# Spatial attentions of a four-layer image kernel: inverse sums spread by transposes, an output projection folded into the value weights, division in place in PSUM

## The chip, the cores and the metric

The kernel runs on one core of a Trainium2 chip. The metric is the time of one execution in microseconds; smaller is better. The core has TensorE (PE in the profile, with its weight loads shown apart as PEld), VectorE (DVE), ScalarE (ACT) and GpSimd (POOL). SyncE (SP) issues most of the DMA transfers, ACT some. All engines run their own instruction streams in order and wait for each other by semaphores.

## The reference, cut to what matters

All data are float32. Four layers run one after the other on `x` of shape (2, 128, 64, 64), so N = 4096 positions for each of two images: a state-space layer (layer 0), an attention over positions with 3x3 convolutions for queries, keys and values and a 1x1 output projection (layer 1), an attention with 1x1 projections (layer 2), and a multi-scale layer (layer 3). The two attentions are what the change touches:

```python
# layer 1
q = conv2d(x, Wq, bq, 1).reshape(b, c, n)
k = conv2d(x, Wk, bk, 1).reshape(b, c, n)
v = conv2d(x, Wv, bv, 1).reshape(b, c, n)
attn = softmax(einsum('bci,bcj->bij', q, k) * c ** -0.5, axis=2)
out = einsum('bij,bcj->bci', attn, v).reshape(b, c, h, w)
out = conv2d(out, Wo, bo, 0)            # 1x1
x = x + out
# layer 2
q, k, v = (einsum('dc,nci->ndi', w_, xf) + b_ for w_, b_ in ((wq, bq), (wk, bk), (wv, bv)))
attn = softmax(einsum('nci,ncj->nij', q, k), axis=-1)
x = gamma * einsum('ncj,nij->nci', v, attn) + x
```

The output projection of layer 1 is linear in the channels, as the values' convolution is, and the softmax's division is a factor for each query.

## The kernel before, in words

Layer 0 is written as 32 chunks of 512 positions (two images, two inner layers, eight chunks); each chunk is 32 slots long. `background(i)` lists by hand which steps are emitted in which slot beside the scan of chunk i: step functions are given to `at(slot, function, ...)`, and within a slot they are emitted in the order listed. The loop over chunks begins at i = -2, so that chunk 0 is prepared ahead. During i = -1 nothing is scanned yet: `load_rest` (slot 1, L175) issues the loads of the raw 3x3 weights of layer 1 (`raws`, three tiles for queries, keys and values) and of the second image; `prepare(1)` is emitted in slot 7 (L156); `fold(k)` in slots 8 to 10 (L190) makes on VectorE, out of a raw weight tile, the weights of a one-dimensional Winograd form of the convolution; `fold_out` (slot 23, L208) writes them to DRAM. The same slots hold the first chunk's own path: silu on ScalarE (slot 11, L332), `xproj` (slot 13), `spread_bc` (slot 14, DMAs through DRAM), `soft_plus` (slot 17), `dt_end` on GpSimd (slot 18), `spread_dtu` (slot 19), `times_b` (slot 26, L389) and then the first scans (L407). Matmul outputs of these steps share two PSUM buffers (`mm`, tag "mm").

The attentions are four runs, `runs = [(0,0),(0,1),(1,0),(1,1)]` as (layer, image). A run has 128 units; eight units make a group of 256 queries (`QG`), 16 groups a run. Each pass `now` of the loop at L904 emits one unit's scores (`score`, L749: two matmuls of 128x512 and one VectorE instruction that copies them out of PSUM and takes their maxima), the products of the unit 14 passes earlier (`product`, L803: four matmuls of 128x256 that accumulate into `po`), and what falls due by `w = now % 8`: exponentials on ScalarE (w 3 and 7), `turn` (w 1, 5 and 3, 7; L776: row sums and reciprocals, a 32x32 block transpose on VectorE, and copies or DMAs that bring the blocks to their places), and the end of a group. Queries, keys and values of layer 1 go through `products` and `outputs` (L647, L668); `values` also turns the values by 128x128 transposes (`turned`, L713).

A group ends like this. `diagonals` (w 2, L811) makes on VectorE two 128x128 diagonal matrices out of the identity and the reciprocals `rec` of the row sums. `spread` (w 3, L816) multiplies a matrix of ones by each, so that the reciprocals lie along the columns and are the same on all partitions; ScalarE copies the result out (`rb`). `divide` (w 5, L832) multiplies `po` by `rb` into an SBUF tile `on`, and in layer 2 adds `gamma * on` to the image. In layer 1, `finish_mm` (w 7, L838) multiplies `on` by the output projection into `p2`, and `finish` (L843) adds `p2` and the bias `bo1` to the image:

```python
dg = sta["dg", it] = sp.tile([P, P], F32, name="dg", tag="dg", bufs=2)
nc.vector.tensor_scalar(dg, ident, sta["rec", r, grp][:, it : it + 1], None, ALU.mult)
nc.tensor.matmul(pr[:, it * P : (it + 1) * P], lhsT=ones, rhs=sta["dg", it], start=True, stop=True)
nc.tensor.matmul(sta["p2", r, grp], lhsT=wa[:, WS_O : WS_O + C], rhs=sta["on", r, grp], start=True, stop=True)
```

`pr` and `p2` share one PSUM buffer (`psm`, tag "m"); `po` has two (`psa`, tag "acc"), and scores two of 128x1024 (`pss`).

Of the kernel before, what the change touches and what calls it, by code (L numbers as in the profile page):

```python
# [6 lines left out]
F32 = mybir.dt.float32  # L7
AF = mybir.ActivationFunctionType
ALU = mybir.AluOpType
# [4 lines left out]
B, C, H, W = 2, 128, 64, 64  # L14
N = H * W
P = 128
# [43 lines left out]
WS_O, WS_Q, WS_K, WS_V, WS_IN, WS_OUT, WS_FUS = 0, 128, 256, 384, 512, 896, 1024  # L60
# [7 lines left out]
def tile_conv_seq(ctx: ExitStack, tc, x, consts, vecs, wemb, wlay, wconv, wdt, wqkv, wsmall, wms, out):  # L68
    nc = tc.nc

    kp = ctx.enter_context(tc.tile_pool(name="const", bufs=1))
# [11 lines left out]
    def rows(ap):  # L83
        return ap.rearrange("p (h w) -> p h w", w=W)
# [15 lines left out]
    ident = kc[:, K_ID : K_ID + P]  # L100
    cm = kc[:, K_CM : K_CM + P]
    ones = kc[:, K_ONE : K_ONE + P]

    def v1(name, i=0):
        return vec[:, VEC[name] + i : VEC[name] + i + 1]
# [10 lines left out]
    with tc.manual_schedule(), ExitStack() as s:  # L116
        wp = layers.enter_context(tc.tile_pool(name="l0w", bufs=1))
        spl = layers.enter_context(tc.tile_pool(name="l0t", bufs=1))
        mm = layers.enter_context(tc.tile_pool(name="l0mm", bufs=2, space=PSUM))
        yp = layers.enter_context(tc.tile_pool(name="l0y", bufs=1, space=PSUM))  # L120
        sp = scans.enter_context(tc.tile_pool(name="l0s", bufs=1, side="right"))
# [3 lines left out]

        we = wp.tile([P, 2, C], F32, name="we")
        nc.sync.dma_start(we, wemb)


        sel = wp.tile([P, 32], F32, name="sel")  # L130
# [14 lines left out]
        def load_layer(l):  # L145
            cw = sp.tile([P, KC + 1, DI], F32, name="cw", tag="h", bufs=5)
            nc.sync.dma_start(cw[:, KC, :], wlay[l][:, :DI])
            nc.sync.dma_start(cw[:, :KC, :].rearrange("p k d -> p (k d)"), wconv[l : l + 1, :].to_broadcast([P, KC * DI]))
            cws.append(cw)
            w = wp.tile([P, NWL - DI], F32, name=f"wl{l}")  # L150
            nc.sync.dma_start(w, wlay[l][:, DI:])
            d = wp.tile([R, DI], F32, name=f"wd{l}")
            nc.sync.dma_start(d, wdt[l])
            wl.append(w), wd.append(d)
# [18 lines left out]
        raws, folded = [], []  # L173

        def load_rest():  # L175
            for which in range(3):
                raw = sp.tile([P, 3, 3, C], F32, name="raw", tag="h", bufs=5)
                nc.sync.dma_start(raw.rearrange("p y x c -> p (y x) c"), wqkv[:, which])
                raws.append(raw)
            for c in range(NCH):  # L180
                load_x(1, c)
# [4 lines left out]
        for c in range(2, NCH):  # L186
            load_x(0, c)
        load_layer(1)

        def fold(which):  # L190

# [301 lines left out]
        def background(i):  # L493

            todo = [[] for _ in range(NSL)]

            def at(t, f, *a):
                todo[t].append((f, a))

            n, p, q, r = i + 1, i - 1, i - 2, i + 2  # L500
            if has(q):
                at(3, gelu, q)
                at(6, ffn_down, q, (0, 1)), at(7, ffn_down, q, (2, 3)), at(9, ffn_add, q)
                at(11, out_mm, q), at(12, out_add, q)
            if has(p):
                at(7, y_out, p, 1), at(7, gate, p)
                at(9, mix_out, p), at(11, mix_add, p)
            if has(n):
                at(0, pu_taps, n, 0, (0, 1)), at(1, pu_taps, n, 0, (2, 3)), at(2, pu_out, n, 0)
                at(3, pu_taps, n, 1, (0, 1)), at(4, pu_taps, n, 1, (2, 3)), at(5, pu_out, n, 1)  # L510
                at(13, xproj, n), at(14, xproj_out, n), at(14, spread_bc, n, 0), at(22, spread_bc, n, 1)
                at(15, dtproj, n, 0), at(16, dtproj, n, 1), at(17, soft_plus, n), at(18, dt_end, n)
            if has(i):
                at(1, pz_mm, i, 0), at(3, pz_out, i, 0)
                at(5, pz_mm, i, 1), at(6, pz_out, i, 1)
            if has(i) or has(n):
                at(11, silu, i, n)
            if i == -1:
                at(1, load_rest), at(7, prepare, 1)
                for k in range(3):  # L520
                    at(8 + k, fold, k), at(23, fold_out, k)
                at(19, spread_dtu, 0), at(26, times_b, 0)
            pair = [(k, second) for k, second in ((p, True), (r, False)) if has(k)]
            if has(r):
                at(10, embed, r), at(11, embed_out, r)
            w, m = {}, len(pair)
            for k, (it, second) in enumerate(pair):
                at(12 + 2 * k, ln_centre, w, k, it)
                at(13 + 2 * k, ln_square, w, k, it)
                at(27, ln_spread, w, k, m), at(28, ln_scale, w, k, it)  # L530
                at(29, ln_shift, w, k, it, second)
            if pair:
                at(17, ln_var, w, m), at(18, ln_eps, w, m), at(19, ln_rs, w, m), at(20, ln_newton, w, m), at(21, ln_step, w, m)
            if has(p):
                for f in range(4):
                    at(30 + f // 2, ffn_up, p, f)
            if has(i):
                at(24, y_out, i, 0)
            return todo
# [34 lines left out]
        wa = wbig.tile([P, NWA], F32, name="wa")  # L574
# [6 lines left out]
        QG = 256  # L581
        NB, NTH = P // 32, N // P // 2
        NU = 8 * N // QG
        LAG = 14
# [7 lines left out]
        runs = [(l, b) for l in range(2) for b in range(B)]  # L592
        sta = {}
# [2 lines left out]
            nc.scalar.activation(dst, src, AF.Identity, bias=bias)  # L596

        def bias(r, which):
            return v1("b" + "qkv"[which] + "12"[runs[r][0]])


# [206 lines left out]
                rhs = sta["pt", r, grp, jt // NTH][:, :, jt % NTH, :]  # L808
                nc.tensor.matmul(sta["po", r, grp], lhsT=sta["vt"][:, jt, :], rhs=rhs, start=(jt == 0), stop=(jt == N // P - 1))  # L809

        def diagonals(r, grp):  # L811
            for it in range(2):
                dg = sta["dg", it] = sp.tile([P, P], F32, name="dg", tag="dg", bufs=2)
                nc.vector.tensor_scalar(dg, ident, sta["rec", r, grp][:, it : it + 1], None, ALU.mult)

        def spread(r, grp):  # L816

            pr = psm.tile([P, QG], F32, name="pr", tag="m")
            for it in range(2):
                nc.tensor.matmul(pr[:, it * P : (it + 1) * P], lhsT=ones, rhs=sta["dg", it], start=True, stop=True)  # L820
            rb = sta["rb", r, grp] = sp.tile([P, QG], F32, name="rb", tag="rb", bufs=2)
            nc.scalar.copy(rb, pr)

        def xg(r, grp):
            l, b = runs[r]
            if l:
                k = QG // W
                return xt[:, b, 1 + grp * k : 1 + (grp + 1) * k, 1 : W + 1]
            cc, i = divmod(grp, 4)
            return xt[:, b, 1 + 16 * cc : 17 + 16 * cc, 1 + i : W + 1 : 4]  # L830

        def divide(r, grp):  # L832
            on = sta["on", r, grp] = sp.tile([P, QG], F32, name="on", tag="on")
            nc.vector.tensor_tensor(on, sta.pop(("po", r, grp)), sta.pop(("rb", r, grp)), ALU.mult)
            if runs[r][0]:
                nc.vector.scalar_tensor_tensor(xg(r, grp), rows(on), v1("gamma"), xg(r, grp), ALU.mult, ALU.add)

        def finish_mm(r, grp):  # L838
            if not runs[r][0]:
                sta["p2", r, grp] = psm.tile([P, QG], F32, name="p2", tag="m")  # L840
                nc.tensor.matmul(sta["p2", r, grp], lhsT=wa[:, WS_O : WS_O + C], rhs=sta["on", r, grp], start=True, stop=True)

        def finish(r, grp):  # L843
            if not runs[r][0]:
                nc.vector.scalar_tensor_tensor(xg(r, grp), sta.pop(("p2", r, grp)).rearrange("p (h w) -> p h w", w=16), v1("bo1"), xg(r, grp), ALU.add, ALU.add)

        def in_turn(f, u0):

            r, u = divmod(now - u0, NU)
            if 0 <= r < len(runs):  # L850
                f(r, u)

        NALL = len(runs) * NU
# [47 lines left out]
        sp = s.enter_context(tc.tile_pool(name="ats", bufs=1, reuse_waits="tile"))  # L901
        psa = s.enter_context(tc.tile_pool(name="atpa", bufs=2, reuse_waits="tile", space=PSUM))
        psm = s.enter_context(tc.tile_pool(name="atpm", bufs=1, reuse_waits="tile", space=PSUM))
        for now in range(NALL + LAG + 10):  # L904
            r, u = divmod(now, NU)
            w = now % 8
            if now < NALL:
# [42 lines left out]
                elif u == LAG:  # L950
                    load(0, LO), load(0, HI)
                    if r == 0:
                        load(1, LO)
            if w == 7:
                in_turn(lambda r, u: finish_mm(r, u // 8), LAG + 9)
            in_turn(product, LAG)
            if w == 7:
                in_turn(lambda r, u: finish(r, u // 8), LAG + 9)
            if w in (3, 7):
                in_turn(lambda r, u: exponentials(r, u // 4), 3)  # L960
            if w in (1, 5):
                in_turn(lambda r, u: turn(r, u // 4, 0), 5)
            if w in (3, 7):
                in_turn(lambda r, u: turn(r, u // 4, 1), 7)
            if w == 2:
                in_turn(lambda r, u: diagonals(r, u // 8), 10)
            if w == 3:
                in_turn(lambda r, u: spread(r, u // 8), 11)
            if w == 5:
# [7 lines left out]
    with ExitStack() as s, tc.manual_schedule():  # L977
        sp = s.enter_context(tc.tile_pool(name="mss", bufs=1, reuse_waits="tile"))
        mm = s.enter_context(tc.tile_pool(name="msmm", bufs=3, reuse_waits="tile", space=PSUM))
# [493 lines left out]
```

## Time and profile before

| what | value |
|---|---|
| median of 3 runs | 4995.87 us (4994.74 to 4996.39) |
| span of the profiled execution | 4994.0 us |
| its own time | not listed beside the span; the three runs lie 0.7 to 2.4 us above the span, the median 1.9 us |
| PE busy | 4661.7 us, 93% of the span |
| DVE busy | 4022.4 us, 81% |
| ACT busy | 2358.4 us, 47% |
| POOL busy | 2335.3 us, 47% |
| mean granted TensorE clock | 0.950 |

The span is cut in 40 slices on the profile's page. Layer 0 takes about the first 2180 us, the attentions the stretch from there to about 4218 us, layer 3 the rest. In layer 0 DVE is at nine tenths or more in nearly all slices and PE at eight to nine; in the attentions PE is at nine tenths or more throughout and DVE at six to eight. "Busy" of a matmul is modelled and holds its latency, so the rate of a row of matmuls is read from the distances between starts in the timeline, and a float32 matmul that isn't a transpose counts as two instructions there.

### The profile page before, as it was taken

What the parts mean: (1) busy time and instruction counts of PE and PEld (TensorE: products, weight loads), DVE (VectorE), ACT (ScalarE), POOL (GpSimd) and SP (SyncE); (2) the same over time, 40 slices, a digit from 0 to 9 for tenths busy, and PEclk for the clock granted to TensorE, in tenths of its full rate; (3) what the DMA queues carried; (4) which work ended last, traced back from release to release, by engine and by line L of the source; (5) the groups of instructions that cost most, each with busy time, mean ns of one, the idle gap of its engine ahead of it and who ended that gap; (6) DMA issues with size and microseconds to landing.
All of it is one profiled execution on the core that took longest, in us unless ns stands there. A gap on an engine that the chain in (4) does not pass through costs nothing.

```text
span 4994.0 us, 48951 instructions
## 1 busy us (share of the span) xinstructions
PE 4661.7 (93%) x14797; PEld 2242.2 (45%) x14797; DVE 4022.4 (81%) x4283; ACT 2358.4 (47%) x3218; POOL 2335.3 (47%) x1974
## 2 busy tenths in 40 slices
PE   6898899899988899899999999999999999999997
PEld 2222222222222222366667766666666666333332
DVE  7999999999999999778886677767776775667776
ACT  4677777777777777532222222233233332323332
POOL 3777777666777777513332233323333332333331
PEclk7889998998999989899999999999999999999998
DMA  6233333332333333224444344434444443000000
GB/s 165 68 69 69 69 71 73 71 69 65 67 67 69 69 70 68 71 57 110 109 109 126 105 111 113 118 97 111 113 98 98 110 114 87 3 7 7 5 7 9
DMA packets 242343, 386.24 MB, mean 77 GB/s; under 512 B 88592, under 2 KB 88992, under 8 KB 233632
## 3 DMA queue, kind: packets, MB, share of 16 engines
q1 hardware_dynamic: 192928, 315.94, 26.1%
q10 hardware_dynamic: 49152, 67.17, 5.4%
q8 instruction: 118, 1.93, 0.2%
q14 instruction: 145, 1.19, 0.1%
HBM read 101.02 MB, written 13.37 MB: 23 GB/s over the span
## 4 chain that ended last, share of the span: by engine, by line
PE 46%; POOL 24%; issue 12%; DVE 9%; DMA 3%; SPq 2%; ACT 2%; ACTq 0%; DVEq 0%; POOLq 0%
POOL h L414 19%; PE po L809 13%; PE pq L759 13%; DVE tr L789 3%; DMA pt<-tr 3%; PE pa L656 2%; PE pf L1130 2%; SPq L800 2%; PE pqkv L1157 2%; PE pw L1216 1%; POOL dtu L374 1%; POOL z L437 1%; PE pb L656 1%; PE pfus L1281 1%; PE psc L1181 1%
## 5 line engine op out<-in xcount | busy, mean ns | idle before, releaser
L796 POOL COPY pt<-tr 32x512 f32<-32x512 f32 x1024 | 648.8, 634 | 1439.2 <-DVE tr L789 704.5
L411 DVE TENSOR_TENSOR_SCAN h<-da,carry,h 128x512 f32<-128x512 f32 x1024 | 1240.7, 1265 | 62.0 <-ACT da L400 31.8
L414 POOL TENSOR_TENSOR h<-h,cb 128x2048 f32<-128x2048 f32 x256 | 1160.8, 4535 | 20.7
L759 PE MATMUL pq<-k,q 128*128 128x512 f32 x2048 | 962.6, 593 | 6.9 <-DVE sc L764 6.9
L809 PE MATMUL po<-pt,vt 128*128 128x256 f32 x4096 | 965.6, 379 | 2.5 <-DMA pt<-tr 2.5
L774 ACT ACTIVATE sc<-sc,nm 128x2048 f32<-128x2048 f32 x256 | 510.5, 1995 | 914.9 <-DVE nm L770 685.8
L809 PEld LDWEIGHTS po<-pt,vt 128*128 128x128 f32 x4096 | 777.9, 190 | 294.8 <-issue 208.3
L764 DVE TENSOR_SCALAR_CACHE_REDUCE sc<-pq 128x1024 f32<-128x1024 f32 x512 | 624.7, 1221 | 315.4 <-PE pq L759 293.8
L400 ACT ACTIVATE da<-dtb,am 128x512 f32<-128x512 f32 x1024 | 681.4, 684 | 220.9 <-DVE h L411 207.6
L789 DVE STREAM_TRANSPOSE tr<-sc 128x2048 f32<-128x2048 f32 x256 | 591.6, 2311 | 65.6 <-DMA pt<-tr 56.3
L393 DVE TENSOR_TENSOR h<-bb,pdu 128x2048 f32<-128x2048 f32 x256 | 581.3, 2271 | 77.6 <-PE py L426 29.4
L426 PE MATMUL py<-h,sel 128*32 128x512 f32 x2048 | 510.8, 642 | 1.6 <-POOL h L414 1.6
L759 PEld LDWEIGHTS pq<-k,q 128*128 128x128 f32 x2048 | 382.9, 190 | 283.0 <-issue 247.2
L387 PE MATMUL pdu<-dtu,fsel 128*128 128x512 f32 x512 | 327.6, 726 | 103.0 <-DVE h L393 100.6
L426 PEld LDWEIGHTS py<-h,sel 128*32 128x32 f32 x2048 | 115.3, 118 | 415.9 <-issue 409.0
L314 PE MATMUL pu<-xn,wu 128*128 128x512 f32 x512 | 246.4, 615 | 7.2 <-ACT u L320 5.5
L387 PEld LDWEIGHTS pdu<-dtu,fsel 128*128 128x128 f32 x512 | 96.6, 215 | 310.2 <-DVE h L393 185.9
L413 POOL COPY carry<-h 128x4 f32<-128x4 f32 x256 | 47.7, 186 | 389.8 <-DVE h L411 389.8
L1223 DVE TENSOR_TENSOR ov<-v,pw 128x2048 f32<-128x2048 f32 x64 | 146.1, 2284 | 62.1 <-PE pw L1216 62.1
L1157 PE MATMUL pqkv<-f,ws 128*128 128x512 f32 x384 | 188.1, 615 | 3.0 <-DVE prod L1174 2.3
L1227 POOL TENSOR_TENSOR ov<-ov 128x2048 f32<-128x2048 f32 x16 | 72.5, 4534 | 235.7 <-DVE ov L1223 235.7
L374 POOL TENSOR_TENSOR dtu<-dt,u 128x1024 f32<-128x1024 f32 x32 | 75.2, 2350 | 188.7 <-ACT dt L368 188.7
(259 smaller groups left out, 5262.2 us busy)
## 6 DMA issues: line engine op xcount, KB each, us to landing
pt<-tr SPq DMA_DIRECT2D x2048, 64.0 KB, 2.0
dtb<-dt SPq DMA_DIRECT2D x1024, 64.0 KB, 2.0
pt<-tr ACTq DMA_DIRECT2D x1024, 64.0 KB, 2.2
bb<-dr SPq DMA_DIRECT2D x128, 256.0 KB, 4.4
cb<-dr SPq DMA_DIRECT2D x128, 256.0 KB, 4.7
uw<-ufold SPq DMA_DIRECT2D x12, 576.0 KB, 4.9
uw<-dkept SPq DMA_DIRECT2D x20, 288.0 KB, 3.1
xt<-in_x SPq DMA_DIRECT2D x16, 256.0 KB, 4.8
```

The costliest lines, as they stand in the source:

```text
L387: nc.tensor.matmul(pdu, lhsT=four(s_ % 4), rhs=st[i]["dtu"][:, s_ // 4, :], start=True, stop=True)
L393: nc.vector.tensor_tensor(h, st[i]["bc", 0], pdu.unsqueeze(1).to_broadcast([P, 4, CH]), ALU.mult)
L400: nc.scalar.activation(da, st[i]["dtb", s_], AF.Exp, scale=am[items[i][1]][:, j, gg, m : m + 1])
L411: nc.vector.tensor_tensor_scan(h[:, m, :], da, h[:, m, :], carries[b, l][:, j, gg, m : m + 1], ALU.mult, ALU.add)
L414: nc.gpsimd.tensor_tensor(h, h, st[i]["bc", 1], ALU.mult)
L426: nc.tensor.matmul(py[r : r + 32, :], lhsT=sel, rhs=st[i]["h", s_ + k][:, m, :], start=(m == 0), stop=(m == 3), tile_position=(0, r),)
L759: nc.tensor.matmul(pq[:, i, :], lhsT=sta["q", r, grp][:, it * P : (it + 1) * P], rhs=sta["k"][:, at : at + CH], start=True, stop=True)
L764: nc.vector.tensor_scalar(dst, pq, 1.0, None, ALU.mult, ALU.max, accum_out=sta["mx"][:, c2 : c2 + 1])
L774: nc.scalar.activation(sc, sc, AF.Exp, bias=nm, scale=scale, accum_out=sm[:, hh : hh + 1])
L789: nc.vector.transpose(tr, sta.pop(("sc", r, blk, hh)).rearrange("p (t r f) -> p r t f", r=NB, f=32))
L796: nc.gpsimd.tensor_copy(dst, src)
L809: nc.tensor.matmul(sta["po", r, grp], lhsT=sta["vt"][:, jt, :], rhs=rhs, start=(jt == 0), stop=(jt == N // P - 1))
```

## The change

In both attentions the inverse sums are spread by a transpose on TensorE of `rec` itself, read with a stride of zero over 128 columns; `diagonals` and its tiles are gone. `divide` multiplies `po` by `rb` in place in PSUM and then adds to the image straight from there, in layer 1 too. `finish_mm`, `finish` and `p2` are gone: the output projection of layer 1 is multiplied into the raw weights of its values' convolution, and into that convolution's bias (`bvo`), by a new step `through_out`, which is emitted in slot 9 of i = -1, after `prepare(1)` and before `fold(1)` and `fold(2)`. One load (`wo`, 64 KB) is added at the head of `load_rest`. The attention loop is two passes shorter.

```diff
         def load_rest():
+            nc.sync.dma_start(wo, wsmall[:, WS_O : WS_O + C])
             for which in range(3):
...
+        def through_out():
+
+            raw = raws[2].rearrange("p y x c -> p (y x) c")
+            for turn in (True, False):
+                for k in range(0, 9, 3):
+                    pv = mm.tile([P, 3, C], F32, name="pv", tag="mm")
+                    for i in range(3):
+                        if turn:
+                            nc.tensor.transpose(pv[:, i, :], raw[:, k + i, :], ident)
+                        else:
+                            nc.tensor.matmul(pv[:, i, :], lhsT=raw[:, k + i, :], rhs=wo, start=True, stop=True)
+                    nc.scalar.copy(raw[:, k : k + 3, :], pv)
+            pb = mm.tile([P, 1], F32, name="pbv", tag="mm")
+            nc.tensor.matmul(pb, lhsT=wo, rhs=v1("bv1"), start=True, stop=True)
+            nc.scalar.copy(bvo, pb)
...
-                at(1, load_rest), at(7, prepare, 1)
+                at(1, load_rest), at(7, prepare, 1), at(9, through_out)
...
         def bias(r, which):
+            if which == 2 and not runs[r][0]:
+                return bvo
...
-        def diagonals(r, grp):
+        def spread(r, grp):
+
+            pr = psm.tile([P, QG], F32, name="pr", tag="m")
+            rec = sta.pop(("rec", r, grp))
             for it in range(2):
-                dg = sta["dg", it] = sp.tile([P, P], F32, name="dg", tag="dg", bufs=2)
-                nc.vector.tensor_scalar(dg, ident, sta["rec", r, grp][:, it : it + 1], None, ALU.mult)
-
-        def spread(r, grp):
-
-            pr = psm.tile([P, QG], F32, name="pr", tag="m")
-            for it in range(2):
-                nc.tensor.matmul(pr[:, it * P : (it + 1) * P], lhsT=ones, rhs=sta["dg", it], start=True, stop=True)
+                nc.tensor.transpose(pr[:, it * P : (it + 1) * P], rec[:, it : it + 1].to_broadcast([P, P]), ident)
...
         def divide(r, grp):
-            on = sta["on", r, grp] = sp.tile([P, QG], F32, name="on", tag="on")
-            nc.vector.tensor_tensor(on, sta.pop(("po", r, grp)), sta.pop(("rb", r, grp)), ALU.mult)
+            po = sta.pop(("po", r, grp))
+            nc.vector.tensor_tensor(po, po, sta.pop(("rb", r, grp)), ALU.mult)
             if runs[r][0]:
-                nc.vector.scalar_tensor_tensor(xg(r, grp), rows(on), v1("gamma"), xg(r, grp), ALU.mult, ALU.add)
-
-        def finish_mm(r, grp):
...
-        def finish(r, grp):
...
+                nc.vector.scalar_tensor_tensor(xg(r, grp), rows(po), v1("gamma"), xg(r, grp), ALU.mult, ALU.add)
+            else:
+                by = po.rearrange("p (h w) -> p h w", w=16)
+                nc.vector.scalar_tensor_tensor(xg(r, grp), by, v1("bo1"), xg(r, grp), ALU.add, ALU.add)
...
-        for now in range(NALL + LAG + 10):
+        for now in range(NALL + LAG + 8):
...
-            if w == 7:
-                in_turn(lambda r, u: finish_mm(r, u // 8), LAG + 9)
             in_turn(product, LAG)
-            if w == 7:
-                in_turn(lambda r, u: finish(r, u // 8), LAG + 9)
...
-            if w == 2:
-                in_turn(lambda r, u: diagonals(r, u // 8), 10)
```

More of the change, by code (lines that the diff above doesn't have):

```diff
@@ L127, in tile_conv_seq @@
         nc.sync.dma_start(we, wemb)
+        wo = wp.tile([P, C], F32, name="wo")
+        bvo = kp.tile([P, 1], F32, name="bvo")
         sel = wp.tile([P, 32], F32, name="sel")
@@ L832, in divide @@
         def divide(r, grp):
-            on = sta["on", r, grp] = sp.tile([P, QG], F32, name="on", tag="on")
-            nc.vector.tensor_tensor(on, sta.pop(("po", r, grp)), sta.pop(("rb", r, grp)), ALU.mult)
+            po = sta.pop(("po", r, grp))
+            nc.vector.tensor_tensor(po, po, sta.pop(("rb", r, grp)), ALU.mult)
             if runs[r][0]:
-                nc.vector.scalar_tensor_tensor(xg(r, grp), rows(on), v1("gamma"), xg(r, grp), ALU.mult, ALU.add)
-        def finish_mm(r, grp):
-            if not runs[r][0]:
-                sta["p2", r, grp] = psm.tile([P, QG], F32, name="p2", tag="m")
-                nc.tensor.matmul(sta["p2", r, grp], lhsT=wa[:, WS_O : WS_O + C], rhs=sta["on", r, grp], start=True, stop=True)
-        def finish(r, grp):
-            if not runs[r][0]:
-                nc.vector.scalar_tensor_tensor(xg(r, grp), sta.pop(("p2", r, grp)).rearrange("p (h w) -> p h w", w=16), v1("bo1"), xg(r, grp), ALU.add, ALU.add)
+                nc.vector.scalar_tensor_tensor(xg(r, grp), rows(po), v1("gamma"), xg(r, grp), ALU.mult, ALU.add)
+            else:
+                by = po.rearrange("p (h w) -> p h w", w=16)
+                nc.vector.scalar_tensor_tensor(xg(r, grp), by, v1("bo1"), xg(r, grp), ALU.add, ALU.add)
         def in_turn(f, u0):
```

## The prediction

> **What bounds the kernel now.** I read the page first, then the engines' busy times by stretches, then the timeline of PE inside a group, the groups of instructions by line, and last the start of the run. Stretches of 100 us in the attentions (columns: stretch, then busy us and count of PE, PEld, DVE, ACT, POOL, granted clock, DMA share, GB/s):
>
> ```profile
> 2350.00:2450.00 100.00, 98.55 (x357) 66.44 (x356) 86.45 (x135) 26.98 (x30) 35.14 (x49) 1.00 0.40 98
> 3450.00:3550.00 100.00, 100.00 (x362) 67.20 (x361) 76.58 (x113) 32.01 (x36) 34.57 (x56) 1.00 0.46 112
> ```
>
> The first lies in run 0, the second in a run of layer 2. PE has no gaps, at full clock; DVE has 14 to 24% to spare. A matmul taken away here shortens the run by its distance between starts; DVE work taken away gives nothing unless PE waits for it. The chain of waits names other engines in run 0 (DVE's block transposes and the DMAs behind them), but with PE at 98.5% there they can hide no more than 1.5%.
>
> The distances, from PE's timeline (start, us, line, count):
>
> ```profile
> 2714.29 1.89 PE L809 MATMUL po<-pt,vt 128*128 128x256 f32 x8
> 2716.02 0.61 PE L820 MATMUL pr<-dg,kc 128*128 128x128 f32 x4
> 2716.46 1.88 PE L759 MATMUL pq<-k,q 128*128 128x512 f32 x4
> ...
> 2728.51 0.59 PE L841 MATMUL p<-on,wa 128*128 128x256 f32 x2
> 2728.95 1.89 PE L809 MATMUL po<-pt,vt 128*128 128x256 f32 x8
> ...
> 2789.62 1.04 PE L719 MATMUL pvt<-kc,vs 128*128 128x128 f32 x8
> ```
>
> `spread` takes 2716.46 - 2716.02 = 0.44 us of PE, `finish_mm` 2728.95 - 2728.51 = 0.44. A matmul is two instructions, a transpose (L719) one: eight run 1.04 us, the last one's 0.27 included, so (1.04 - 0.27)/7 = 0.11 us each, as an instruction of `spread` does ((0.61 - 0.275)/3 = 0.11).
>
> The groups of the attentions that the change touches (busy us, mean ns of one, then the idle time before them):
>
> ```profile
> L814 DVE TENSOR_SCALAR dg<-kc,rec 128x128 f32<-128x128 f32 x124 | 51.8, 460 | 0.0
> L820 PE MATMUL pr<-dg,kc 128*128 128x128 f32 x248 | 39.4, 278 | 0.6 <-DVE dg L814 0.4
> L834 DVE TENSOR_TENSOR on<-po,rb 128x256 f32<-128x256 f32 x64 | 24.7, 386 | 15.9 <-PE po L809 15.9
> L845 DVE SCALAR_TENSOR_TENSOR xt<-p,vec,xt 128x256 f32<-128x256 f32 x32 | 21.6, 676 | 0.0
> L836 DVE SCALAR_TENSOR_TENSOR xt<-on,vec,xt 128x256 f32<-128x256 f32 x32 | 21.0, 657 | 1.1
> L841 PE MATMUL p<-on,wa 128*128 128x256 f32 x64 | 19.6, 387 | 3.5 <-DVE on L834 3.5
> ```
>
> The start, where `through_out` goes, from the timelines of PE, ACT and DVE:
>
> ```profile
> 37.07 0.38 PE L163 MATMUL pa<-an,fsel 128*128 128x32 f32 x2 [0.34 <-DVE am L166]
> 37.74 1.10 PE L239 MATMUL pe<-xt,we 128*128 128x512 f32 x2 [0.30 <-PE pa L163]
> ...
> 34.81 1.28 ACT L334 ACT_TABLE_LOAD   x1
> 45.29 0.58 ACT L347 COPY dbl<-pd 40x512 f32<-40x512 f32 x1 [2.49 <-PE pd L343]
> 69.89 1.91 ACT L400 ACTIVATE da<-dtb,am 128x512 f32<-128x512 f32 x3 [6.65 <-DMA dtb<-dt]
> ...
> 57.72 0.54 DVE L206 COPY uhi<-raw 128x384 f32<-128x384 f32 x1
> 58.35 2.29 DVE L393 TENSOR_TENSOR h<-bb,pdu 128x2048 f32<-128x2048 f32 x1
> ```
>
> Here ACT starts the table load of the first silu the moment its queue is free, and the first `times_b` (L393) waits for the last fold alone; the second scans wait for a DMA of `dtb`.
>
> **The change part by part**, against the span of 4994.0; the median of the runs stands 1.9 us above it.
>
> *Spread.* 64 groups, each with two matmuls (0.44) replaced by two transposes (2 x 0.11 = 0.22): 64 x 0.22 = -14.1 us on PE's path. The weight load of a transpose takes 141 ns against 190 and overlaps; with a stride of zero, the nearest row is L287's load of a broadcast column, 185. Bounds: 0 if it becomes two passes, -14.1 as taken from L719.
>
> *Diagonals.* 128 x 0.46 = 59 us of DVE fall away beside PE: nothing, except where PE waited. Lines L820 and L841 waited in all 2.3 us for `dg` and 3.5 for `on` (run 0 mainly): -5.8, at most; the reciprocals that the transposes now need are written two units earlier, nearly 7 us, so no wait takes the first one's place. What is late next in run 0 is the copy out of a score (L764), for which PE waited 2.0 us.
>
> *Output projection.* 32 groups of layer 1 x 0.44 = -14.0 us of PE. No other instruction grows: the folded weights have the shape of the old ones. `pr` no longer waits for `p2` to leave its shared buffer; nobody waited there.
>
> *Divide in place.* DVE's product writes PSUM instead of SBUF. No DVE row of before writes PSUM. ACT's do: 128x512 takes 684 ns into PSUM (L400) and 690 into SBUF (L320), so 0; the far bound is the product's own time over again, +0.39 each, 25 us of DVE in all. Both lie under DVE's 14 to 24%. The addition reads PSUM in layer 2 as it did in layer 1 (676 against 657). In layer 1 it moves from w 7 to w 5, where it stands behind a block transpose: copy 1.22 + sums 0.3 + transpose 2.31 + product 0.39 + addition 0.68 = 4.9 us before the next unit's copy, against 3.44 us a unit. Scores have two buffers, so PE needs that copy only at the second unit after; 1.22 + 4.9 is 6.1 of some 8.6 us there. I take 0; at worst, some 0.3 us in each of run 0's 16 groups, +5. ACT's `rb` copy is as before, and `po` held 0.7 us longer is next wanted a whole group later. At the very end (product at 4217.97) some +0.1.
>
> *Attention in sum:* -14.1 - 14.0 - 5.8 = -33.9; bounds -15 and -36.
>
> *Through_out.* Nine transposes, nine matmuls (18 instructions), six copies of 128x384 and a bias column, once, but in order on PE and ACT. PE can't begin before `prepare`'s last matmuls, at about 37.7 instead of `pe`. ACT's silu, free at 34.81, now stands behind the seventh copy. A copy of 128x384 is about 0.48 us (0.373 for 256 columns, 0.586 for 512). PE's 27 instructions are 3.0 us at full clock, 6.0 at half; the rows of 40 to 44 us show a granted clock of 0.50. With two buffers the groups of three run as: PE, hand-off, copy, and the third PE group waits for the first copy. Walking that gives an end at 42.4 at full clock, 44.4 at half; bounds 41.3 (all copies but the last hidden) and 49.4 (nothing overlaps, half clock). I take 44.4, since the clock was half: silu +9.6. Before, ACT waited 0.4 for `pe`, which now is early: +9.2 for `dbl` (L347), and behind it for everything that SP has in its queue: `dr`, `bb`, the first `dtb`, `cb`, six `ufold` writes, the second `dtb`. The last `ufold` no longer waits for the last fold, -0.5. So the second scans move from 70.6 to about 79. The folds hide none of it: fold(2) ends at 58.26 as before or up to 3.4 us sooner (its three slow instructions, 1.6 to 1.8 instead of 0.55, run while GpSimd does), and the first `times_b` then waits for `pdu` instead. Behind the second scans, layer 0 is one chain in a fixed order with DVE at 93%, which gives nothing back. +8.7, bounds +5.5 and +13.7.
>
> The load of `wo` (SP, 0.45 us ahead of the raw weights, which land near 30) is hidden: `through_out` wants them at 37.7.
>
> Sum: -33.9 + 8.7 = -25.2: span 4968.8, time 4970.7.
>
> A rule that speaks against this: the Trainium skill, "TensorE: Matmul & The Clock Gate", Part 4, says that transposes do not count as activity for the clock gate, and Part 1 that an idle window of about 3.4 us halves the clock. This trace agrees with the idle window (0.91 over 3225 to 3245, behind a PE gap of 3.7 us); on transposes it is silent, since no row has two of them alone between matmuls. By the page read at its worst, each pair would cost half a window, an estimate of 1.7 us, 109 us in 64 groups, where the rows give -14.1.
>
> **The rivals.**
>
> *A: the start is free.* If something else were late there, the attention's -33.9 stands alone: 4962.0. For it: DVE had been the last at 58 us. Against: `dtb` at 69.9, which hangs on the same ACT queue.
>
> *B: half the gain.* Either run 0 is held by DVE and its DMAs, as its chain says (16 of the groups lose 0.22 + 0.44 and the waits: 16.4 back, 4987), or the broadcast transpose takes two passes (14.1 back, 4985). Against the first: PE at 98.5%; against the second: L719.
>
> *C: a longer start.* Hand-offs at their bound: +13.7, 4975.7; it is inside the forecast's range.
>
> *D: slower, by the clock.* The clock drops to half for a while at each pair of transposes. A drop of 3.4 us (the width of the dips behind 0.91 in 20 us) costs 1.7 us of PE's path; 64 of them +109, with the rest 4970.7 + 109 = 5080. It decides from 25.2/64 = 0.4 us a group, a drop at one group in four. For it: one dip stands where transposes come in rows of eight (3290). Against: it has a PE gap of 2.4 us too, the dips at 3225 and 3705 have gaps of 3.7 us and no transpose, and 0.22 us of transposes stands among 28 us of matmuls. A second way to the same side is the moved addition stalling PE: 32 groups x 0.8 us would do, 4996; the 2.0 us of waiting for L764 speak against it.
>
> **How the numbers follow.** Forecast (with C, 4964 to 4979): 0.67. A: 0.09. B: 0.12. D and the moved addition: 0.12. Where PE's clock falls in layer 0 (0.90 on the mean) can shift a few us either way; that is inside the ranges. No change is within 0.2%, 10 us, of 4995.87: 4985.9 to 5005.9, about what a measurement can tell. Faster takes the forecast, A and a little of B (those under 4985.9), 0.78; same the rest of B and half-strength stalls, 0.11; slower D, 0.11. The range 4957 to 4988 leaves out D and the stalls, and reaches over A and B.
>
> **What would show it.** Right: in steady groups two L820-like transposes 0.11 apart and a group of layer 1 0.66 us shorter, of layer 2 0.22; no `p2`; DVE down by some 59 us with no change of the span from it; PE still 100% in 3450 to 3550; the first silu's table load near 44, the second scans near 79. Wrong: a granted clock below 1.00 in steady stretches, PE waiting for L764 by more than 10 us in all, four instructions where two transposes are expected, or the start of the scans unmoved.

## The result and the profile after

The changed kernel takes 4976.71 us (median of 5 runs, 4975.69 to 4980.28) against 4995.81 of the kernel before beside it: ratio 0.9962, interval 0.995 to 0.9974, so 19.1 us or 0.38% faster. The span of its profiled execution is 4973.9 us against 4994.0. Forecast were 4970.7 us and a range of 4957 to 4988: the direction and the size hold, the gain is three quarters of the forecast.

Two kinds of stretch, run 0 and layer 2 (columns as before):

```profile
2350.00:2450.00 100.00, 99.03 (x356) 66.48 (x355) 86.14 (x128) 26.71 (x30) 35.98 (x50) 1.00 0.41 102
3450.00:3550.00 100.00, 100.00 (x355) 66.34 (x354) 74.70 (x108) 32.67 (x36) 34.08 (x56) 1.00 0.46 112
```

PE is the bound as before, at full clock, although each group now has its pair of transposes. DVE lost its 128 diagonals, some 2 us of 100 in layer 2, and the stretch is no less full on PE for it. Over all the attentions DVE's busy time falls from 1515.1 to 1470.4 us: 45 us, not the 59 that the prediction added up.

PE's timeline around a spread of layer 1, and the groups that changed (lines have moved; L837 is the transposes, L851 the division, L856 and L853 the additions of layers 1 and 2):

```profile
2811.28 1.89 PE L830 MATMUL po<-pt,vt 128*128 128x256 f32 x8
2813.01 0.38 PE L837 MATMUL pr<-kc,rec 128*128 128x128 f32 x2
2813.23 1.88 PE L780 MATMUL pq<-k,q 128*128 128x512 f32 x4
```

```profile
L851 DVE TENSOR_TENSOR po<-po,rb 128x256 f32<-128x256 f32 x64 | 25.7, 401 | 15.9 <-PE pwt L1005 15.9
L837 PE MATMUL pr<-kc,rec 128*128 128x128 f32 x126 | 24.1, 273 | 0.0
L856 DVE SCALAR_TENSOR_TENSOR xt<-po,vec,xt 128x256 f32<-128x256 f32 x32 | 21.9, 684 | 1.1
L837 PEld LDWEIGHTS pr<-kc,rec 128*128 128x128 f32 x126 | 17.3, 137 | 6.6
L853 DVE SCALAR_TENSOR_TENSOR xt<-po,vec,xt 128x256 f32<-128x256 f32 x32 | 15.5, 485 | 1.1
```

The spread is two instructions and takes 2813.23 - 2813.01 = 0.22 us of PE, as forecast; the weight loads of these transposes, with the broadcast column, are no longer than those of the others (137 ns against 140 at L740). From one spread to the next, a steady group of layer 1 takes 27.77 us instead of 28.43 and one of layer 2 28.20 instead of 28.43: 0.66 and 0.23 us less, as forecast. The division into PSUM takes 401 ns against 386.

The start, from ACT's and DVE's timelines:

```profile
43.99 1.28 ACT L353 ACT_TABLE_LOAD   x1
53.05 0.58 ACT L366 COPY dbl<-pd 40x512 f32<-40x512 f32 x1 [2.42 <-PE pd L362]
78.11 1.91 ACT L419 ACTIVATE da<-dtb,am 128x512 f32<-128x512 f32 x3 [9.35 <-DMA dtb<-dt]
62.05 2.29 DVE L412 TENSOR_TENSOR h<-bb,pdu 128x2048 f32<-128x2048 f32 x1 [7.03 <-DMA bb<-dr]
78.84 4.81 DVE L430 TENSOR_TENSOR_SCAN h<-da,carry,h 128x512 f32<-128x512 f32 x4 [5.12 <-ACT da L419]
```

The table load of the first silu stands at 43.99 instead of 34.81, `dbl` at 53.05 instead of 45.29, and the second scans begin at 78.84 instead of 70.62: 8.2 us later. DVE, which used to be the last at 58 us, now idles 7 us for the DMA of `bb`.

Cut at the second scans (of the first chunk's second set), the first score and the start of the last division, the profiled executions stand like this, one of each kernel; the kernels from the third row on are those of the experiments. "Clock" is what PE lost in the attentions to half clock: half the length of the half-clock windows in the trace's clock record.

| kernel | second scans | to first score | attentions | clock | attentions less clock | rest |
|---|---|---|---|---|---|---|
| before | 70.6 | 2114.1 | 2033.3 | 10.2 | 2023.1 | 776.0 |
| after | 78.8 | 2116.1 | 2000.6 | 6.8 | 1993.8 | 778.4 |
| spread alone | 69.9 | 2114.1 | 2020.9 | 15.4 | 2005.5 | 777.9 |
| fold alone | 80.7 | 2115.5 | 2024.5 | 15.4 | 2009.1 | 778.4 |
| without the step | 70.4 | 2114.0 | 2006.3 | 11.9 | 1994.4 | 775.8 |
| turned thrice | 80.9 | 2113.1 | 2004.0 | 10.2 | 1993.8 | 781.6 |
| no turn | 79.0 | 2113.4 | 2004.1 | 10.2 | 1993.9 | 778.3 |
| projection late | 69.5 | 2112.3 | 2005.8 | 11.9 | 1993.9 | 776.2 |
| addition later | 78.6 | 2115.3 | 2000.7 | 8.5 | 1992.2 | 778.3 |
| both | 72.3 | 2114.4 | 2002.6 | 10.2 | 1992.4 | 776.0 |

The column of layer 0 and the last one scatter by 4 and 6 us, in kernels that are alike or nearly alike there. The last one isn't free of pattern: it is 778.3 to 781.6 in the five kernels with the added work at the start, and 775.8 to 776.2 in four of the five without it (777.9 in spread alone). Time lost to half clock more than accounts for the 2.4 us between before and after (20.5 us there before, 23.9 after), but why it falls so is open. The attentions scatter by 6 us between the five kernels with the changed kernel's attention code; less the clock's share, these lie within 0.6 us. So after against before is +8.2 (start), +2.0 (layer 0, within its scatter), -29.3 (attentions), -3.4 (clock in the attentions, within the 6.8 to 11.9 of kernels with the same code), +2.4 (layer 3, open): -20.1, the difference of the spans.

### The profile page after: what moved, and what is told of

Same layout as the page of the kernel before. It is cut to its first block, busy times and chain, and to the rows that moved or that the text cites. A ratio compares the mean times of both kernels' runs of the same rounds, so it can differ in the third digit from the quotient of the medians.

```text
span 4973.9 us, 48435 instructions
## 1 busy us (share of the span) xinstructions
PE 4643.1 (93%) x14634; PEld 2218.0 (45%) x14634; DVE 3975.5 (80%) x4155; ACT 2361.8 (47%) x3225; POOL 2331.1 (47%) x1974
## 4 chain that ended last, share of the span: by engine, by line
PE 46%; POOL 25%; issue 12%; DVE 8%; DMA 4%; SPq 3%; ACT 3%; ACTq 0%; POOLq 0%; DVEq 0%
POOL h L433 19%; PE pq L780 13%; PE po L830 13%; DVE tr L810 3%; SPq L821 3%; DMA pt<-tr 3%; PE pa L677 2%; PE pf L1135 2%; PE pqkv L1162 2%; PE pw L1221 1%; POOL dtu L393 1%; POOL z L456 1%; PE pb L677 1%; PE pfus L1286 1%; PE psc L1186 1%
## 5 line engine op out<-in xcount | busy, mean ns | idle before, releaser
L830 PEld LDWEIGHTS po<-pt,vt 128*128 128x128 f32 x4096 | 777.9, 190 | 309.5 <-issue 227.5
```

## The experiments

**Spread alone.** The kernel before, with

```diff
...
-                nc.tensor.matmul(pr[:, it * P : (it + 1) * P], lhsT=ones, rhs=sta["dg", it], start=True, stop=True)
+                nc.tensor.transpose(pr[:, it * P : (it + 1) * P], rec[:, it : it + 1].to_broadcast([P, P]), ident)
...
-                in_turn(lambda r, u: diagonals(r, u // 8), 10)
```

> The kernel before with one part of the change alone: the inverse sums are spread by transposes, the diagonals are gone; projection and division are as before. Theory (PE's distance between starts is the price): the attention's stretch (first score to last division) gets 64 x 0.22 = 14.1 us shorter, and up to 2.3 us more from the waits for the diagonals: 2017 to 2019 us instead of 2033.3; layer 0 and layer 3 as before within 2 us; time 4979 to 4982. Rival (a wait for the reciprocals or for ScalarE's copy takes the place): the stretch gets less than 7 us shorter, and PE shows waits before the transposes.

Measured: 4984.67 us against 4997.09, ratio 0.9976 (0.9966 to 0.9985). The time lies 3 us above the range expected and the stretch, 2020.9, 2 us above its own. The attentions are 12.4 us shorter, 17.6 less the clock's share, more than the 14.1 of the distances. The distances tell why: summed from PE's timeline over the 64 groups, the old spread took 31.1 us, not 64 x 0.44 = 28.2, since in eight groups of run 0 (and in the very last group, 0.81) its second matmul waited for the second diagonal and the pair took 0.65 to 0.89. The new one takes 0.22 in all but the first group. PE's waits for the diagonals, 2.3 us, are gone, but those for the copies of scores are longer than before (6.9 there):

```profile
PE pq L759 <- DVE sc L764: 9.4, 11, 2.0
```

All of that growth lies before 2320 us, while run 0's pipeline fills (7.9 instead of 5.4); in its later groups they are 1.6 instead of 1.5.

**Fold alone.** The changed kernel, with the old spread, additions that read `on`, and

```diff
...
-            nc.vector.tensor_tensor(po, po, sta.pop(("rb", r, grp)), ALU.mult)
+            on = sp.tile([P, QG], F32, name="on", tag="on")
+            nc.vector.tensor_tensor(on, sta.pop(("po", r, grp)), sta.pop(("rb", r, grp)), ALU.mult)
```

> The changed kernel with the old spread (diagonals, matrix of ones) and with the division into SBUF; the projection stays folded into the value weights. Theory: the attention's stretch gets 32 x 0.44 = 14.0 us shorter, and up to 3.5 us more from the waits for the division: 2016 to 2019 us; the second scans start near 79 us instead of 70.6 and the first score 8 to 10 us later; time 4986 to 4990. Rival (the start is absorbed in layer 0): first score within 3 us of before, time near 4979.

Measured: 4999.89 us, ratio 1.0004 (0.9994 to 1.0013). The start is delayed as said, more so here (ACT's timeline):

```profile
45.23 1.28 ACT L353 ACT_TABLE_LOAD   x1
80.00 1.91 ACT L419 ACTIVATE da<-dtb,am 128x512 f32<-128x512 f32 x3 [9.96 <-DMA dtb<-dt]
```

The attentions less clock gain 14.0, the 32 projections (14.3 by their distances), and no more: the waits for the division, 3.5 us, are gone, but those for score copies have come (6.9 before):

```profile
PE pq L780 <- DVE sc L785: 11.7, 17, 2.0
```

Here the growth lies mostly in run 0's later groups (5.4 instead of 1.5), where the waits for the division had been. The expectation of 4986 to 4990 failed by 10 us. The start costs 10.1 us in this profile, and the attentions lose 5.2 us more to half clock than before, which lies outside the 6.8 to 11.9 us of the changed kernel's code and isn't explained; no gain is left that could be measured. The folding, as placed, pays for itself and nothing beyond.

**Without the step.** The changed kernel without `through_out` and `bvo`, so without the output projection of layer 1:

```diff
-                at(1, load_rest), at(7, prepare, 1), at(9, through_out)
+                at(1, load_rest), at(7, prepare, 1)
```

> The changed kernel without the step that folds the projection into the values' weights and bias (left out of the computation: the output projection of layer 1); the load of its weights stays. Theory (the start's delay goes through to the end one for one): second scans at 70 to 72 us, first score within 2 us of before (2184.7), attention 2000 to 2002 us as in the changed kernel, time 4963 to 4967. Rival (layer 0 lost its 10 us by chance or for another reason, such as where the clock falls): first score still 5 us or more later than before, time above 4969.

Measured: 4969.02 us, ratio 0.9947 (0.9932 to 0.9961): 28.1 below the kernel before beside it, where the changed kernel was 19.1 below. By the medians the step costs 9 us; the two intervals (0.9932 to 0.9961 here, 0.995 to 0.9974 there) just overlap, so the profiles' start has to carry the claim. The time is 2 us above the range expected; this profile lost 11.9 us of the attentions to half clock, the changed kernel's 6.8. DVE's start is that of before, fold and all:

```profile
57.47 0.54 DVE L225 COPY uhi<-raw 128x384 f32<-128x384 f32 x1
58.10 2.29 DVE L412 TENSOR_TENSOR h<-bb,pdu 128x2048 f32<-128x2048 f32 x1
...
70.40 4.81 DVE L430 TENSOR_TENSOR_SCAN h<-da,carry,h 128x512 f32<-128x512 f32 x4 [2.46 <-ACT da L419]
```

The second scans begin 8.4 us earlier than in the changed kernel, and the first score comes at 2184.4 (before: 2184.7; changed: 2194.9). So nothing of the delay is absorbed by layer 0, as the theory had it.

**Turned thrice.**

```diff
-            for turn in (True, False):
+            for turn in (True, True, True, False):
```

> The changed kernel with the raw value weights turned three times instead of once, which gives the same weights: 18 transposes and six copies more in the step at the start. Theory: the first silu's table load moves from 44.0 to about 48 us (a transposed group of three costs 0.66 us on PE at half clock and about as much with hand-offs, six of them 4 us), the second scans and the first score move by the same 4 us, time 4979 to 4982. Rival (DVE's idle time at the start or slack in layer 0 takes it): first score moves by less than 1.5 us, time 4975 to 4978.

Measured: 4981.43 us, ratio 0.9969 (0.9958 to 0.9981), 15.7 below before. From ACT's and PE's timelines:

```profile
46.68 1.28 ACT L353 ACT_TABLE_LOAD   x1
38.09 4.04 PE L201 MATMUL pv<-kc,raw 128*128 128x128 f32 x18 [0.25 <-DVE am L168]
42.38 0.93 PE L201 MATMUL pv<-kc,raw 128*128 128x128 f32 x6 [0.24 <-ACT raw L204]
43.55 2.49 PE L203 MATMUL pv<-wo,raw 128*128 128x128 f32 x18 [0.24 <-ACT raw L204]
```

The silu moves by 2.7 us and the second scans by 2.1, not by 4: half the clock was assumed, and the clock came back to full at 41.7 us. The time rises (15.7 below before instead of 19.1), but the first score of this profile lies 0.9 us earlier than in the changed kernel, which is what the rival said, within the scatter of layer 0. The span is 5.7 us longer than the changed kernel's, and the table says where: +2.1 at the start, -3.0 in layer 0, +3.4 of clock in the attentions, +3.2 in layer 3. So the time agrees with the range expected, but this run decides nothing beyond the start itself.

**No turn.** The values' raw weights are laid out in DRAM with their channels exchanged, so that the first round falls away:

```diff
-            for turn in (True, False):
+            for turn in (False,):
```

> The changed kernel, with the raw value weights laid out in DRAM with their channels exchanged, so that the step at the start needs no turn: nine transposes and three copies fewer there. Theory (the step's length passes to the end one for one): the first silu's table load comes near 41.5 us instead of 44.0, second scans and first score 2.5 us earlier than in the changed kernel, time some 2.5 us below it. Rival (the start is held by something else, such as the DMA queue): second scans stay at 78 to 80 us.

Measured: 4976.38 us against 4996.24, ratio 0.9957 (0.9945 to 0.997). The expectation failed:

```profile
43.10 1.28 ACT L353 ACT_TABLE_LOAD   x1
38.32 4.18 PE L203 MATMUL pv<-wo,raw 128*128 128x128 f32 x18
```

The silu gains 0.9 us and the second scans nothing (79.0), so the rival's sign came true, though not by the DMA queue. The 18 matmul instructions took 4.18 us here, 3.61 in the changed kernel: the clock was half from 36.7 to 53.8, there only from 39.2 to 42.6. Shorter work at half clock came to nearly the same end, and the 0.9 us went at `pc`, a matmul behind the silu, which took 2.07 us here and 1.13 there; `dbl` stands at 53.18 against 53.05. The start's price is thus a matter of where the clock stands as much as of the instruction count.

**Projection late.** The values' raw weights lie in DRAM as in the run without the turn, and nothing of the projection stays at the start: the folded but unprojected weights go to DRAM as before, and in chunks 1 to 3 of layer 0 six tiles each are loaded, multiplied and written back:

```diff
-                at(1, load_rest), at(7, prepare, 1), at(9, through_out)
+                at(1, load_rest), at(7, prepare, 1)
...
+            if 1 <= i <= 3:
+                at(8, vo_load, i - 1)
+                at(19, vo_mm, i - 1, 0), at(21, vo_copy, i - 1, 0)
+                at(21, vo_mm, i - 1, 1), at(23, vo_copy, i - 1, 1)
+                at(29, vo_store, i - 1)
+            if i == 4:
+                at(21, bias_out)
```

> As the run without the turn, but nothing of the projection stays at the start: the values' weights are folded for the convolution and written to DRAM unprojected, and the 18 tiles are loaded, multiplied and written back in chunks 1 to 3 of layer 0, six a chunk, in slots where few other steps use the two shared PSUM buffers. Theory: the first silu at 34.8, second scans at 70 to 71, first score within 3 us of the kernel before; attention as in the changed kernel; time 8 to 10 us below the changed kernel, as the run without the step. Rival (the work costs as much in layer 0, where PE is 90% and DVE 93% busy): 36 matmul instructions and six copies, some 4 to 8 us, come back between second scans and first score, and the time is less than 5 us below the changed kernel.

Measured: 4965.86 us, ratio 0.9939 (0.9927 to 0.9952): 30.4 us below before, and 11 below the changed kernel as each stands to its own runs of before. It beats both kernels: its five runs, 4964.2 to 4968.6, all lie below those of the changed kernel. The second scans are back, and others waited for the moved work 2.5 us in all (DVE's scans, then PE's instructions of that work and who waited for it):

```profile
69.54 4.81 DVE L436 TENSOR_TENSOR_SCAN h<-da,carry,h 128x512 f32<-128x512 f32 x4 [0.45 <-ACT da L425]
```

```profile
L202 PE MATMUL pv<-wo,vo x36: 275/276/583, 161.9 to 295.0; 128*128 128x128 f32 x36
...
who waited for it (us, times):
  PEld pr L312: 2.5, 3
```

From second scans to first score it is 2112.3 us, the shortest in the table: the 36 instructions cost nothing that can be seen in layer 0 beside its scatter of 4 us.

**Addition later.** In layer 1 the addition goes back to w 7 (the last group of a run keeps it at w 5), to see if its place behind the block transpose made PE wait for the score copies:

```diff
-            else:
-                by = po.rearrange("p (h w) -> p h w", w=16)
+            elif grp == NU // 8 - 1:
+                finish(r, grp, True)
...
             in_turn(product, LAG)
+            if w == 7:
+                in_turn(lambda r, u: finish(r, u // 8), LAG + 9)
```

> The changed kernel with the addition of layer 1 two units later (w 7, as in the kernel before), the multiplication in place staying at w 5. Theory (the moved addition made PE wait for the copies of scores in run 0): PE's waits for the score copies fall from 12.5 to 9 to 10 us, the attention's stretch without clock losses from 1993.8 to about 1991, time 2 to 3 us lower. Rival (the waits come from the end of the old waits for diagonals and division, which PE reaches sooner): they stay at 12 us or more and the stretch at 1993 to 1995.

Measured: 4975.4 us, ratio 0.9959 (0.9946 to 0.9973). PE's waits in the attentions, this kernel:

```profile
PE pq L780 <- DVE sc L785: 12.2, 11, 2.0
```

Fewer waits, the same sum: where the changed kernel waits twice in a group of run 0 (0.2 and 0.5 us), this one waits once (0.65). On the waits the rival holds: they don't belong to the addition's place. The stretch less clock, 1992.2, lies between what the two said; it is 1.6 us shorter, 1.4 with both changes, which may be real, but the times don't resolve it.

**Both.** The two edits together.

> Both: the projection of the weights moved into chunks 1 to 3 of layer 0, and the addition two units later. Theory: the two gains add, 10 to 13 us below the changed kernel, near 4965. Rival: as for each alone; no more than 5 us below.

Measured: 4967.52 us, ratio 0.9944 (0.9931 to 0.9956), 28.7 below before and 9.6 below the changed kernel: no more than the late projection alone. The gains don't add; the addition brings nothing that can be measured.

## Why the prediction was right, and where a term was off

The bound, the direction and the mechanism held: PE's distances between starts were the price in the attentions, and the start passed on to the end. What the prediction had no term for (layer 0 +2.0, clock -3.4, layer 3 +2.4) comes to +1.0 in sum, and that this is so little is luck. The terms against the traces:

- *Spread, -14.1:* measured -17.0 (31.1 to 14.1, the wait for a score copy in the first group left out). The distance of 0.44 was read in a steady group; half of run 0's groups had a longer pair, which holds a wait between the two matmuls that the list of waits put on the weight loads.
- *Output projection, -14.0:* measured -14.3 from the distances, -14.0 by the fold alone.
- *Waits for `dg` and `on`, -5.8:* this is the term that failed. They went, but PE's waits for the score copies grew by as much. PE's waits in the attentions of the kernel before:

```profile
PE pq L759 <- DVE sc L764: 6.9, 10, 2.0
...
PE p L841 <- DVE on L834: 3.5, 7, 0.8
PE pr L820 <- DVE dg L814: 2.3, 2, 1.8
```

and after:

```profile
PE pq L780 <- DVE sc L785: 12.5, 18, 2.0
```

  That is +5.6 against -5.8: nothing gained. Half of the growth (5.4 to 8.2) lies before 2320 us, while run 0's pipeline fills, half in its later groups. I had named the copies of scores as what is late next, but with a wait of 2.0 us, where the view of before has 6.9 in all (2.0 is its longest), and sized them at 0 to 5 for the moved addition; the run with the addition later shows the same sum without it. Of the prediction's signs of being wrong, this is the one that came true: PE waits for score copies for more than 10 us in all. The two single parts show the exchange: with the diagonals' waits gone, PE waits longer for score copies while the pipeline fills; with the division's gone, in the later groups. What sets the time of these copies stays open. DVE's whole load in run 0 (86% busy) isn't shown to: spread alone took the diagonals off DVE there, and the waits of the later groups stayed as they were (1.6 and 1.5).
- *Attentions in sum, -33.9:* -29.3 less clock. The terms as measured make -31.5 (-17.0 - 14.3 - 5.8 + 5.6); +1.0 is a longer wait for the block copies (2.5 to 3.5), and +1.2 is not found.
- *Division in place, 0:* right; 401 against 386 ns, and no PE wait behind it. The addition of layer 2 even takes 485 ns instead of 657.
- *Through_out, +8.7:* silu at 43.99 (44.4 said), second scans +8.2, 9 us by the run without it. Of its working some pieces were wrong: the first `times_b` waited for the DMA of `bb` and not for `pdu`; the clock was half for only 3.4 us of the walk, not all of it, which added to the walk's own end at full clock, 42.4, comes to 42.4 + 3.4/2 = 44.1; and `dbl` moved by 7.8, not 9.2, because `pc` in front of it ran at full clock (1.13 us) where before it ran at half (2.08).

Of the rivals, the free start (A) fell with the run without the step: 9 us. Half the gain (B) fell: from its second spread to its fifteenth run 0 takes 394.0 us instead of 403.9, 0.76 a group and so no less than the 0.66 of the steady groups, and the transposes take 0.11 us each. The clock (D) fell: half-clock windows in the attentions are 13.7 us long in all after and 20.5 before, and its second way, the moved addition, fell with the run that puts it back. The Trainium skill's sentence that transposes do not count as activity ("TensorE: Matmul & The Clock Gate", Part 4) does not agree with the run turned thrice: from 38.09 to 42.1 us PE did nothing but transposes, and its clock rose from half to full at 41.7.

## What to carry to other kernels

Where one engine runs without gaps, count its instructions by the distance between starts, and book the waits that an edit removes at nothing until it is clear what the engine meets next: here the same 6 us came back at the neighbouring wait. A preparation step that is cheap in itself can eat most or all of the gain of what it prepares (10 of 14 us in the run with the fold alone) if it stands in order ahead of the work that feeds the first result; its instructions cost nothing that shows beside a scatter of 4 us once they stood in slots behind that point. And one profile's stretch should be freed of its half-clock windows before a difference of 5 us is read from it.

## What was not expected

- The addition of layer 2 reads `po` from PSUM in 485 ns, where the same 128x256 from SBUF took 657. In layer 1 the addition read PSUM before, too, and stays at 684 (676); in the run with the fold alone it reads `on` from SBUF and takes 871, while layer 2's is back at 660. So in both layers the same addition is 0.17 to 0.19 us shorter with its first input in PSUM.
- The same 18 matmul instructions of the start took 4.18, 3.61 and 2.49 us in three kernels, by the place of the half-clock windows. PE was busy without a gap in the windows from 39.2 to 42.6 (after) and from 38.3 to 41.7 (turned thrice), and the clock was full behind them. Without the turn PE was busy for 2.98 us of the window from 36.7 to 40.1 and 3.05 of the next one, and the clock stayed at half. How full a window has to be doesn't come out of these traces: behind the last half-clock window of that run, 50.4 to 53.8, with 2.74 us busy, the clock was full.
